# Cross-attention with image prompts: the gram by balanced column strips, the queries two chunks at once with a contraction split in row halves

## The chip, the cores and the metric

The kernel runs on one core of a Trainium2 chip. The core has a matrix engine (TensorE, in the profile PE for its matmuls and PEld for its weight loads), a vector engine (VectorE, DVE), a scalar engine (ScalarE, ACT), GpSimd (POOL) and SyncE (SP), which here only starts DMA transfers. TensorE multiplies a stationary tile (the weights) with a moving one and adds into one of eight PSUM banks; a bank has 128 partitions of 512 float32 values each. It can be used as one array of 128x128, as column strips of 64 or 32 columns, or as row strips. The metric is the device time of one execution in microseconds (us).

## What is computed

Eight batches of 112 rows with 320 channels attend, with 20 heads of 16 channels, to 371 text tokens of 512 features, and beside these to 4 prompt tokens, whose logits get the cosine between the text that a row attended to and the prompt. Everything is float32.

```python
q = heads(hidden_states @ W_q)
k_t = heads(text_ehs @ W_k)
v_t = heads(text_ehs @ W_v)
probs_t = softmax(einsum('bhsd,bhtd->bhst', q, k_t) * attn_scale)
text_out = einsum('bhst,bhtd->bhsd', probs_t, v_t)
attn_scores = einsum('bhsd,bhnd->bhsn', q, heads(ip_ehs @ W_k_ip)) * attn_scale
qsem = l2norm(einsum('bhst,bte->bhse', probs_t, text_ehs))
sem = einsum('bhse,bne->bhsn', qsem, l2norm(ip_ehs))
probs_ip = softmax(attn_scores + 0.5 * sem) * spatial_mask[None, None, :, None]
ip_out = einsum('bhsn,bhnd->bhsd', probs_ip, heads(ip_ehs @ W_v_ip))
out = (text_out + ip_out) @ W_out + b_out + hidden_states
```

## The kernel before

The norm of `qsem` is not taken from `qsem` itself. For each batch the kernel forms the **gram**, the inner products of all 375 tokens with one another (371 text tokens and the 4 normalised prompts), and multiplies the probabilities with it. As the gram is symmetric, only the part on and right of the diagonal is used: it is doubled, and its diagonal blocks are halved again by a table of halves and ones. The gram, one column of ones and 16 channels of values stand side by side in the tile `u`, so that one set of matmuls per head (`product`, L696, the bulk of TensorE's work) gives the squared norm's terms, the prompts' products and the attended values.

A batch takes these steps. `transposed_context` brings the tokens into `ctxT` (features on partitions; for batches after the first VectorE does it, L396, and GpSimd copies the four prompts behind the text, L384). `gram` (L458 to L476) runs over three chunks of 128, 128 and 119 tokens. In each it runs over four slices of the 512 features (e), and for each e over four column strips of TensorE, 32 tokens each. Strip p takes the block q of the chunk that the table `DEAL` gives it. For e = 0 every strip covers the whole width of the chunk's bank (which starts the sums of all columns); for e > 0 only from its own block on. `doubled` copies the bank to the tile `ug` times two with one ScalarE instruction (L454), and GpSimd multiplies the diagonal part with the table `half` (L455). `gram_to_groups` (L482) moves `ug` to `u` by DMA, four transfers for a block, and `values_to_dram` (L558), `values_to_groups` (L567) and `placed` (L614, GpSimd) bring the values beside it through DRAM. `keys` (L494, and L511 for the last 64 channels, in two column halves) and `values` (L533) are projections of the tokens.

`project_queries` serves one batch first (batch 0) and then the pairs [1,2], [3,4], [5,6] and [7]. It transposes x (L331; ScalarE copies it to `xT`, L334; GpSimd fills the unused rows of the last chunk with zeros, L322), and then makes one chunk of 128 channels per step, three steps (L339): three matmuls of 128 rows over 224 columns (112 for a single batch) and two VectorE scalings into `qm` (L348). The contraction has 320 rows, two of 128 and one of 64, filled up with zeros; the third chunk has 64 channels, which stand twice side by side in the weights.

The attention runs in 40 groups, five per batch and four heads each. Scores (L648) run two groups ahead; `probabilities` takes the row maximum on VectorE (L661, `nmx`), the exponential on ScalarE (L665, `p`), the prompts' logits (L667, `ipl`) and sends the result to `xg` by a DMA per head (L672, on SP). `transposed` turns it on VectorE (L684, `xgT`), and `product` multiplies. After that VectorE (L749) and ScalarE (L723) reduce the product's banks.

Groups run in pairs, and in the middle of each pair stands `behind(n)`: there the other work is put into TensorE's queue by hand, a few steps at a time, with one name in the list `turn` for each PSUM bank that these steps use. `qd` is a pool of four banks, shared with the products; `mm` and `sc` have two each. The order of all five engines is the order of the program, nothing is reordered by a scheduler. In the even batches 0, 2, 4 the work of the next pair of queries is spread over three places: in group 2, three transpositions and the first query step between two steps of values; in group 4, the second query step in front of the keys (and for batches 2 and 4 `finish`, `f`, whose output projection is L852 and whose sum into `ob` on VectorE, L858, frees its bank), the gram of the batch after, and the next transposition of x's probabilities, `tr`; in group 1 of the odd batch, the third query step. Batch 6 makes pair [7]: one query step in group 2, two in group 4. Between the two `tr` of a place stand the gram steps in the program, and SP's queue takes the DMAs of all these in the order in which they were issued.

Of the kernel before, what the change touches and what calls it, by code (L numbers as in the profile page):

```python
# [8 lines left out]
F32 = mybir.dt.float32  # L9
# [11 lines left out]
def kernel(  # L21
# [50 lines left out]
    DEAL = ((0, 1, 2, 3), (3, 2, 1, 0), (0, 1, 2, 3))  # L72
# [97 lines left out]
    half = const.tile([P, 2, P], F32, tag="half", name="half")  # L170
# [38 lines left out]
    def more_constants():  # L209
        halves(1)  # L210
        nc.gpsimd.memset(wo_sb[REST:, FULL, :], 0.0)
        for at in attn_ring:
            nc.gpsimd.memset(at[:, C:], 0.0)
# [100 lines left out]
    def project_queries(bs):  # L314
# [7 lines left out]
        nc.gpsimd.memset(xT[REST:, FULL, :], 0.0)  # L322
        for i in range(NC):
            cn = min(P, C - i * P)
            if bs[0] == 0:

                ps = ps_qd.tile([P, 512], F32, tag="qd", name=f"ps_x_0_{i}")
            else:
                ps = bank(f"ps_x_{bs[0]}_{i}", spare=bs[0] > 1 and i > 0)
            for j, b in enumerate(bs):  # L330
                nc.tensor.transpose(  # L331
                    ps[:cn, j * S : (j + 1) * S], x_sb[:, b, i * P : i * P + cn], ident[:S, :S]
                )
            nc.scalar.copy(xT[:cn, i, : n * S], ps[:cn, : n * S])  # L334
            yield
        for i in range(NC):
            ps = bank(f"ps_q_{bs[0]}_{i}")
            for j in range(NC):
                nc.tensor.matmul(  # L339
                    ps[:, : n * S],  # L340
                    wq_sb[:, j, i * P : (i + 1) * P],
                    xT[:, j, : n * S],
                    start=(j == 0),
                    stop=(j == NC - 1),
                )
# [81 lines left out]
    def first_gram():  # L427
# [3 lines left out]
        for c in range(NT):  # L431
# [4 lines left out]
            for r in range(c + 1):  # L436
# [8 lines left out]
                if c == NT - 1:  # L445
                    doubled(banks[r], r, 0)
                yield

    def doubled(ps, c, h):
# [5 lines left out]
        nc.gpsimd.tensor_tensor(g[:, :k], g[:, :k], half[:, h, :k], ALU.mult)  # L455

    def gram(b):
# [3 lines left out]
        for c in range(NT):  # L461
            t0 = c * P
            ps = bank(f"ps_g_{b}_{c}")
            for e in range(NE):
                for p, q in enumerate(DEAL[c]):

                    s0 = q * RG if e > 0 else 0
                    nc.tensor.matmul(  # L468
                        ps[p * RG : (p + 1) * RG, s0 : T - t0],
                        ctxT[:, e, t0 + q * RG : t0 + (q + 1) * RG],  # L470
                        ctxT[:, e, t0 + s0 : T],
# [3 lines left out]
            doubled(ps, c, c % 2)  # L475
# [699 lines left out]
    def behind(n):  # L1175
# [34 lines left out]
        elif b % 2 == 0 and g == 2:  # L1210
            turn[:] = ["qd"] * (6 + (b == 0)) + ["mm"]
# [13 lines left out]
        elif b % 2 == 0 and nb < B - 1:  # L1225
            turn[:] = ["qd"] * (4 + (b > 0)) + ["mm", "mm"]
            turned(b + 2)
            q(nb)
# [15 lines left out]
        elif b % 2 == 0:  # L1244
            turn[:] = ["qd"] * 4 + ["mm"]
            q(nb, 2)
# [181 lines left out]
```

## Time and profile before

| | us |
|---|---|
| median of three runs | 416.45 (415.63 to 416.67) |
| the profiled execution | 416.37 |
| its span in the profile | 414.6 |
| TensorE busy, matmuls | 407.2 |
| VectorE busy | 325.1 |
| ScalarE busy | 188.2 |
| GpSimd busy | 114.0 |

The granted clock of TensorE was 1.0 throughout. The profile takes one execution; its time lies 1.8 us above its span, which counts from the first instruction to the last. In its rows L12 is a line of the kernel, PE ps_g L468 a matmul into the tile ps_g at line 468, and what stands in square brackets is how long the engine stood idle before, and what released it. A row like "4.64 PE ps_g L468 x71" in the chain of waits is a stretch of 4.64 us that the chain spends on 71 such instructions one after another. A float32 matmul is recorded as two instructions of TensorE. Rows of L339 are the queries, L468 the gram, L696 the products, L533 and L494 values and keys.

### The profile page before, as it was taken

To read this page: it belongs to the slowest core of one execution; us is meant where nothing else is said; L and a number is where in the kernel's file an instruction comes from. 1 tells how busy PE (TensorE), PEld (TensorE's weight loads), DVE (VectorE), ACT (ScalarE), POOL (GpSimd) and SP (SyncE) were. 2 spreads that over 40 slices of the span, in tenths; PEclk is the share of its full clock that TensorE was granted. 3 is DMA by queue.
4 is the path that set the end of the run, shared out by engine and by line. 5 is a ranking of instruction groups with operands and counts; after the bars stand their busy time and mean duration, and the time that the engine had idled before them with its cause. 6 is when DMAs were issued, how large, how long until landed. Compare 5 with 4: busy or idle time off the path is not lost.

```text
span 414.6 us, 14048 instructions
## 1 busy us (share of the span) xinstructions
PE 407.2 (98%) x5609; PEld 317.4 (77%) x5609; DVE 325.1 (78%) x694; ACT 188.2 (45%) x652; POOL 114.0 (27%) x266
## 2 busy tenths in 40 slices
PE   8999999999999999999999999999999999999996
PEld 7867777777778786879687877778777878687884
DVE  4256787868888877887898897897888897878975
ACT  3254343336443752515553654333633464336763
POOL 4203112020351351021161135002134126004680
PEclk9999999999999999999999999999999999999999
DMA  7777965986584846578676576566756345666310
GB/s 245 167 197 241 186 167 135 208 196 166 136 184 111 189 117 169 139 167 177 161 164 139 160 158 159 161 167 154 173 147 160 91 123 133 170 151 192 100 48 28
DMA packets 58244, 64.64 MB, mean 156 GB/s; under 512 B 19061, under 2 KB 52041, under 8 KB 58180
## 3 DMA queue, kind: packets, MB, share of 16 engines
q1 hardware_dynamic: 57150, 61.47, 60.3%
q0 software_dynamic: 464, 1.56, 1.7%
q8 instruction: 44, 0.72, 0.8%
q10 hardware_dynamic: 566, 0.72, 0.5%
q14 instruction: 20, 0.16, 0.1%
HBM read 19.03 MB, written 5.22 MB: 59 GB/s over the span
## 4 chain that ended last, share of the span: by engine, by line
PE 95%; DMA 2%; ACT 1%; DVE 1%; POOL 0%; issue 0%; SPq 0%; DVEq 0%
PE ps_qd L696 44%; PE ps_v L533 13%; PE ps_k L494 10%; PE ps_g L468 8%; PE ps_s L648 6%; PE ps_q L339 4%; PE ps_o L852 3%; PE ps_k L511 3%; PE ps_g L438 1%; DMA xg<-p 1%; DMA ct<-in_ctx_dram 1%; PE ps_c L408 1%; PE ps_x L331 0%; POOL shared L738 0%; PE ps_o L948 0%; PE ps_a L843 0%
## 5 line engine op out<-in xcount | busy, mean ns | idle before, releaser
L696 PE MATMUL ps_qd<-u,xgT 32*112 32x40 f32 (+11 forms) x3840 | 217.1, 351 | 1.6 <-DVE xgT L684 1.0
L696 PEld LDWEIGHTS ps_qd<-u,xgT 32*112 32x112 f32 x3840 | 178.1, 172 | 37.7 <-issue 5.5
L684 DVE STREAM_TRANSPOSE xgT<-xg 128x768 f32<-128x768 f32 (+1 forms) x63 | 123.7, 1979 | 11.1 <-DMA xg<-p 9.6
L665 ACT ACTIVATE p<-ps_s,nmx 112x371 f32<-112x371 f32 x160 | 85.7, 585 | 60.8 <-DVE nmx L661 59.5
L661 DVE TENSOR_REDUCE nmx<-ps_s 112x1 f32<-112x371 f32 x160 | 77.3, 535 | 34.8 <-PE ps_s L648 32.8
L614 POOL COPY u<-vr 128x64 f32<-128x64 f32 x120 | 26.9, 237 | 210.7 <-PE ps_qd L696 127.6
L749 DVE CUSTOM_DVE_ANT_0 p<-ps_qd,p 112x371 f32<-112x371 f32 x152 | 73.4, 539 | 13.1 <-ACT pvs L723 8.3
L648 PE MATMUL ps_s<-kT,qm 32*112 32x375 f32 (+1 forms) x320 | 60.9, 485 | 0.0
L533 PE MATMUL ps_v<-wv_sb,ctxT 128*128 128x320 f32 x192 | 56.1, 438 | 0.3 <-ACT kT L501 0.3
L723 ACT COPY pvs<-ps_qd 112x21 f32<-112x21 f32 x152 | 21.8, 198 | 56.3 <-DVE ss L749 49.7
L533 PEld LDWEIGHTS ps_v<-wv_sb,ctxT 128*128 128x128 f32 x192 | 35.3, 190 | 14.7 <-ACT kT L501 1.2
L494 PE MATMUL ps_k<-ctxT,wk_sb 128*128 128x371 f32 x128 | 43.6, 484 | 0.0
L494 PEld LDWEIGHTS ps_k<-ctxT,wk_sb 128*128 128x128 f32 x128 | 23.0, 190 | 13.2 <-issue 1.3
L468 PE MATMUL ps_g<-ctxT 128*32 128x119 f32 (+11 forms) x672 | 33.0, 343 | 0.0
L468 PEld LDWEIGHTS ps_g<-ctxT 128*32 128x32 f32 x672 | 26.2, 109 | 7.4 <-issue 4.6
L648 PEld LDWEIGHTS ps_s<-kT,qm 32*112 32x112 f32 x320 | 27.7, 171 | 5.2 <-ACT p L665 0.4
L396 DVE STREAM_TRANSPOSE ctxT<-ct 128x512 f32<-128x512 f32 x21 | 22.3, 1072 | 6.2 <-DMA ct<-in_ctx_dram 6.2
L540 ACT COPY vext<-ps_v 128x320 f32<-128x320 f32 x24 | 10.2, 426 | 36.3 <-PE ps_v L533 33.9
L667 ACT COPY ipl<-ps_s 112x4 f32<-112x4 f32 x140 | 24.2, 173 | 0.0
L454 ACT ACTIVATE ug<-ps_g 128x375 f32<-128x375 f32 (+2 forms) x24 | 9.1, 378 | 23.3 <-PE ps_g L468 12.5
L455 POOL TENSOR_TENSOR ug<-ug,half 128x128 f32<-128x128 f32 (+1 forms) x24 | 10.6, 449 | 30.3 <-ACT ug L454 30.3
L501 ACT COPY kT<-ps_k 128x371 f32<-128x371 f32 x16 | 7.5, 470 | 22.6 <-PE ps_k L494 22.3
(147 smaller groups left out, 313.5 us busy)
## 6 DMA issues: line engine op xcount, KB each, us to landing
xg<-p SPq DMA_DIRECT2D x159, 162.3 KB
u<-ug SPq DMA_DIRECT2D x128, 99.0 KB
ct<-in_ctx_dram SPq DMA_DIRECT2D x28, 176.0 KB
vip<-vipd SPq DMA_DIRECT2D x7, 560.0 KB
vr<-vd SPq DMA_DIRECT2D x20, 120.0 KB
vd<-vext SPq DMA_DIRECT2D x14, 160.0 KB
vd<-vext SPq DMA_DIRECT2D x28, 40.0 KB
out_dram<-ob SPq DMA_DIRECT2D x7, 140.0 KB
```

Of the source, the lines that this page charges most:

```text
L396: nc.vector.transpose(ctxT[:, :, c * P : (c + 1) * P].rearrange("p e (j i) -> p j e i", i=RG), ct[:, some, :].rearrange("p j (k e) -> p j ...
L468: nc.tensor.matmul(ps[p * RG : (p + 1) * RG, s0 : T - t0], ctxT[:, e, t0 + q * RG : t0 + (q + 1) * RG], ctxT[:, e, t0 + s0 : T], start=(e ...
L494: nc.tensor.matmul(ps[:, :TT], wk_sb[:, e, i * P : (i + 1) * P], s["ctxT"][:, e, :TT], start=(e == 0), stop=(e == NE - 1),)
L533: nc.tensor.matmul(ps[:, :C], ctxT[:, e, c * P : (c + 1) * P], wv_sb[:, e, :], start=(e == 0), stop=(e == NE - 1),)
L614: nc.gpsimd.tensor_copy(region(b, c)[:, :, UV - c * P :], s["vr"][:, c * QN : (c + 1) * QN, g, :])
L648: nc.tensor.matmul(ps[:S, :w], qm[a * RG : (a + 1) * RG, i, r, j * S : (j + 1) * S], s["kT"][a * RG : (a + 1) * RG, i, :w], start=True, st ...
L661: nc.vector.tensor_reduce(nmx, ps[:S, :TT], AX.X, ALU.max, negate=True)
L665: nc.scalar.activation(p, ps[:S, :TT], AF.Exp, bias=nmx)
L667: nc.scalar.copy(s["ipl"][:, groups[g][a], :], ps[:S, TT:T])
L684: nc.vector.transpose(xT[:, j : j + n].rearrange("p j (k q) -> p q j k", q=QN), xg[:, :, j * RG : (j + n) * RG].rearrange("p q (j k) -> p ...
L696: nc.tensor.matmul(banks[a][:S, j * RG : UW], xT[a * RG : (a + 1) * RG, j, :S], region(b, c)[a * RG : (a + 1) * RG, p, q * RG :], start=(j ...
L749: nc.vector.tensor_tensor_reduce(out=p, in0=ps[:S, :TT], in1=p, scale=1.0, scalar=0.0, op0=ALU.mult, op1=ALU.add, accum_out=s["ss"][:, h : ...
```

## The change

There are two parts.

*The gram.* Every strip now starts at its own block for e = 0 as well, so no strip covers columns left of its block, and `DEAL` gives the blocks of the second and third chunk to other strips. Since the columns left of a strip's block are no longer written, `doubled` copies in four pieces: the columns that all strips have, with all partitions, and three pieces of 32 partitions for what is left of them. The table `half` has a slice for each chunk in place of two. The first batch's gram has no strips and keeps the single copy, under the name `doubled_whole`. With the other order of blocks the values of a batch go to DRAM in 1 + 3 + 2 transfers for the three chunks, in place of 1 + 4 + 1.

*The queries of the pairs.* The first two chunks are made in one step, in two banks: two full matmuls for each, and then the last 64 rows of the contraction as two matmuls with 64 rows, the upper half of the array's rows for one bank and the lower half for the other. For this the last 64 rows of the weights and of `xT` are there twice, in both partition halves: GpSimd copies the weights once, ScalarE copies `xT` once per pair, and the fill with zeros is left out. The third chunk is made for both batches of the pair side by side: each batch has its own column half of the array, 64 channels by 112 columns, with its own row half for the last 64 rows, and VectorE scales it with four instructions over 64 partitions and 112 columns in place of two over 128 and 224. For the single batch of the last pair only the last contraction is cut to 64 rows.

As two chunks are now one step, the step in group 4 goes: group 2 makes both chunks (seven `qd` banks in `turn` in place of six), group 4 begins with the step that followed. For pair [7] the third chunk is made there alone.

```diff
-    DEAL = ((0, 1, 2, 3), (3, 2, 1, 0), (0, 1, 2, 3))
+    DEAL = ((0, 1, 2, 3), (3, 2, 0, 1), (1, 2, 3, 0))
...
     def more_constants():
         halves(1)
+        nc.gpsimd.tensor_copy(wq_sb[REST:, FULL, :], wq_sb[:REST, FULL, :])
+        halves(2)
...
             nc.scalar.copy(xT[:cn, i, : n * S], ps[:cn, : n * S])
+            if i == FULL and bs[0] > 0:
+                nc.scalar.copy(xT[REST:, i, : n * S], ps[:REST, : n * S])
             yield
+        both = []
         for i in range(NC):
             ps = bank(f"ps_q_{bs[0]}_{i}")
+            if i < FULL and bs[0] > 0:
+                both.append(ps)
+                for j in range(FULL):
+                    nc.tensor.matmul(
+                        ps[:, : n * S],
+                        wq_sb[:, j, i * P : (i + 1) * P],
+                        xT[:, j, : n * S],
+                        start=(j == 0),
+                        stop=False,
+                    )
+                if i < FULL - 1:
+                    continue
+                for m, ps in enumerate(both):
+                    own = slice(m * REST, (m + 1) * REST)
+                    nc.tensor.matmul(
+                        ps[:, : n * S],
+                        wq_sb[own, FULL, m * P : (m + 1) * P],
+                        xT[own, FULL, : n * S],
+                        start=False,
+                        stop=True,
+                    )
...
+            if i == FULL and bs[0] > 0 and n > 1:
+                w = n * S // 2
+                for j in range(NC):
+                    for h in range(2):
+                        k = slice(h * REST, (h + 1) * REST) if j == FULL else slice(P)
+                        nc.tensor.matmul(
+                            ps[h * REST : (h + 1) * REST, :w],
+                            wq_sb[k, j, FULL * P : C],
+                            xT[k, j, h * w : (h + 1) * w],
+                            start=(j == 0),
+                            stop=(j == NC - 1),
+                        )
...
             for j in range(NC):
+                k = slice(REST) if j == FULL and bs[0] > 0 else slice(P)
...
+    def doubled(ps, c, deal=DEAL[0], h=0):
...
+        common = (QN - 1) * RG
+        nc.scalar.mul(g[:, common:], ps[:, common : T - t0], 2.0)
+        for p, q in enumerate(deal):
+            if q < QN - 1:
+                own = slice(p * RG, (p + 1) * RG)
+                nc.scalar.mul(g[own, q * RG : common], ps[own, q * RG : common], 2.0)
+        nc.gpsimd.tensor_tensor(g[:, :k], g[:, :k], half[:, h, :k], ALU.mult)
...
     def gram(b):
...
                 for p, q in enumerate(DEAL[c]):
-
-                    s0 = q * RG if e > 0 else 0
                     nc.tensor.matmul(
-                        ps[p * RG : (p + 1) * RG, s0 : T - t0],
+                        ps[p * RG : (p + 1) * RG, q * RG : T - t0],
                         ctxT[:, e, t0 + q * RG : t0 + (q + 1) * RG],
-                        ctxT[:, e, t0 + s0 : T],
+                        ctxT[:, e, t0 + q * RG : T],
...
         elif b % 2 == 0 and g == 2:
-            turn[:] = ["qd"] * (6 + (b == 0)) + ["mm"]
+            turn[:] = ["qd"] * (7 + (b == 0)) + ["mm"]
...
         elif b % 2 == 0 and nb < B - 1:
-            turn[:] = ["qd"] * (4 + (b > 0)) + ["mm", "mm"]
+            turn[:] = ["qd"] * (3 + (b > 0)) + ["mm", "mm"]
             turned(b + 2)
-            q(nb)
...
         elif b % 2 == 0:
-            turn[:] = ["qd"] * 4 + ["mm"]
-            q(nb, 2)
+            turn[:] = ["qd"] * 3 + ["mm"]
+            q(nb)
```

37 lines of the change are left out of this document (29 added, 8 removed).

## The prediction

> **What bounds the kernel now.** I read the page's table of engines and its chain of work that ended last, then that chain as a list in order of time, then the groups by shape, and at last the timelines of three stages.
>
> ```profile
> PE 407.2 (98%) x5609; PEld 317.4 (77%) x5609; DVE 325.1 (78%) x694; ACT 188.2 (45%) x652; POOL 114.0 (27%) x266
> ...
> PE 95%; DMA 2%; ACT 1%; DVE 1%; POOL 0%; issue 0%; SPq 0%; DVEq 0%
> PE ps_qd L696 44%; PE ps_v L533 13%; PE ps_k L494 10%; PE ps_g L468 8%; PE ps_s L648 6%; PE ps_q L339 4%; PE ps_o L852 3%; PE ps_k L511 3%; PE ps_g L438 1%; DMA xg<-p 1%; DMA ct<-in_ctx_dram 1%; PE ps_c L408 1%; PE ps_x L331 0%; POOL shared
> ```
>
> TensorE is the path: 95% of the chain and 407 of 414.6 us. A us taken off PE is a us off the kernel, unless PE then stands waiting for what the other engines deliver. The change touches the gram (8%) and the queries (4%). Their stages, from the chain in order of time (start, duration):
>
> ```profile
> 31.46 4.64 PE ps_g L468 x71
> ...
> 61.90 1.14 PE ps_q L339 x6
> 63.03 2.15 PE ps_v L533 x8
> ...
> 75.88 1.33 PE ps_q L339 x6
> ...
> 80.31 4.64 PE ps_g L468 x69
> ...
> 89.97 0.41 issue
> ...
> 97.33 1.33 PE ps_q L339 x6
> 98.66 1.40 PE ps_k L511 x15
> ...
> 117.76 2.35 PE ps_v L533 x8
> ...
> 355.76 0.66 PE ps_q L339 x6
> ...
> 369.28 1.52 PE ps_q L339 x12
> ```
>
> Each matmul is two instructions ("passes"). Eight passes of 320 columns take 2.15 us, so a column costs 2.15/2560 = 0.84 ns. A query pass of 224 columns is 1.14/6 = 0.19 us, one of 112 columns 0.66/6 = 0.11. The same work right after work in another tile shape is dearer: 1.33 against 1.14, 2.35 against 2.15. **A change of tile shape** into 128x128 thus costs 0.19 to 0.20 us. Into the 64-column shape of the last keys: 8 turns of 186 columns at 0.84 ns are 1.25, the row says 1.40, so 0.15.
>
> **The gram (seven times, five of them not in the list above, all 4.64).** The group of its widest pass:
>
> ```profile
> L468 PE MATMUL ps_g<-ctxT 128*32 128x375 f32 x98 | 18.9, 485 | 0.0
> ```
>
> 98 = 7 x 14: four strips x two passes of the first e at the full width, and 3 x 2 more of strip 0. Adding each strip's own passes over the three chunks, strip 0 is longest before: 8 x 375, then 2 x 247 + 6 x 151, then 8 x 119, 5352 columns or 4.50 us; with 0.14 for the shape this is the measured 4.64. Had each set of four passes waited for its widest, it would be 8 x (375 + 247 + 119) = 5928 columns, 4.98 us, which is more than the row. So strips run ahead of one another and the longest sum decides. Afterwards strips 0 and 3 have 8 x (375 + 151 + 87) and 8 x (279 + 215 + 119), both 4904 columns. That is 448 columns, 0.38 us, less: **7 x 0.38 = -2.6 us**.
>
> What it adds is on ACT: four copies in place of one.
>
> ```profile
> L454 ACT ACTIVATE ug<-ps_g 128x119 f32<-128x119 f32 x8 | 2.2, 270 | 3.5 <-PE ps_g L468 2.6 <-PE ps_g L438 0.5 <-POOL attn L213 0.4
> L282 ACT COPY kv<-ps_kv 32x160 f32<-32x160 f32 x1 | 0.3, 284 | 0.0
> L667 ACT COPY ipl<-ps_s 112x4 f32<-112x4 f32 x140 | 24.2, 173 | 0.0
> ```
>
> The last chunk's 0.27 us becomes four of between 0.17 and 0.28, some 0.9 us. Its bank is wanted again by the second pair of scores, over a us into the products, except in the prologue, where a score of the first pair takes it: between 0 and 0.7 us, once. I take 0.1, as ACT is 45% busy and copies back to back overlap at their ends.
>
> **The queries of pairs [1,2], [3,4], [5,6].** They have three places, shown for the first pair; the other two have the same lengths 98 and 196 us later.
> - Stage of group 2 (61.90): 6 passes become 8 full ones and, for the two K = 64 ends, 2 turns of two passes side by side: 10 x 0.19. The 64-row shape has no row here. Below, its entry is free; above, it costs what 128x128 costs, 0.20. I take 0.19, since all shape changes measured lie at 0.15 to 0.20. The values behind it pay their way back, 2.35 for 2.15. So 1.90 + 0.19 + 0.20 - 1.14 = +1.15. That the row halves run at once is seen only of 32-row strips: the page's group of products has 3840 passes of 351 ns in 217 us of busy time. If the two halves went one after the other, it is 0.38 more.
> - Stage of group 4 (75.88): the step goes, the shape change stays with what follows: 0.19 - 1.33 = -1.14.
> - Next batch, group 1 (97.33): 6 passes of 0.19 plus entry become six turns of 112 columns, two at once in column halves, as the last keys' passes are (16 in 1.40): 6 x 0.11 and two shape changes of 0.1 to 0.15, 0.87. So -0.46; between -0.7 (changes free) and 0 (halves in turn).
>
> Together -0.45 each, **-1.4**. Pair [7] pays the same switches over 112 columns: 0.66 becomes 10 x 0.11 + 0.19 and +0.2 behind it (+0.8), the 1.52 of twelve passes becomes 6 x 0.11 and two or three switches (-0.4): **+0.4**. PE alone: **-3.6 us**.
>
> Beside the path: DVE's scalings of the third chunk go from 2 to 4 instructions, the extra ACT copy of xT's tail replaces a POOL fill and has the 2.15 us of values ahead of the queries as cover, and the values go out in six DMAs per batch as before.
>
> ```profile
> L348 DVE TENSOR_SCALAR qm<-ps_q,emask 128x224 f32<-128x224 f32 x18 | 7.2, 445 | 2.7 <-PE ps_q L339 2.7
> L348 DVE TENSOR_SCALAR qm<-ps_q,emask 128x112 f32<-128x112 f32 x12 | 3.3, 326 | 5.1 <-PE ps_q L339 5.1
> ```
>
> 4 x 0.33 - 2 x 0.45 = 0.4 us of DVE, with the keys and values of 100 to 107 us over it.
>
> **What is given back.** In the stage of group 4 the change takes 1.14 + 0.38 = 1.5 us of PE work away, and that work covers a chain of softmax rows, DMAs, transpositions and the output sum. Its length does not change; it starts from scores made just after the group 2 stage, which now ends 1.15 us later. First batch, SP's queue, then DVE and PE:
>
> ```profile
> 55.64 4.05 SPq L672 DMA_DIRECT2D xg<-p  x4
> ...
> 79.48 3.66 SPq L672 DMA_DIRECT2D xg<-p  x4
> 83.19 2.07 SPq L136 DMA_DIRECT2D ct<-in_ctx_dram  x4
> ```
>
> ```profile
> 87.35 1.58 DVE L684 STREAM_TRANSPOSE xgT<-xg 128x768 f32<-128x768 f32 x1 [3.44 <-DMA xg<-p]
> ...
> 89.67 0.57 ACT L665 ACTIVATE p<-ps_s,nmx 112x371 f32<-112x371 f32 x1 [4.30 <-DVE nmx L661]
> ...
> 90.39 1.06 PE L696 MATMUL ps_qd<-u,xgT 32*112 32x392 f32 x5 [0.41 <-POOL u L614]
> ```
>
> SP issues without a pause from 55.64 to 85.26 (the first, eighth and last of nine groups), so the xg data that DVE waits 3.44 us for does not come earlier. Behind that transposition stand the row maxima, and the exponential behind them (to 90.24) frees a bank of the products at 90.39; the row names POOL, whose copy was done earlier. PE is idle there already (89.97, 0.41). PE's lead there is 0.38 (first gram) - 1.15 + 1.14 + 0.38 = 0.75, and I count 0.7 as lost.
>
> Third batch:
>
> ```profile
> 165.97 4.26 SPq L672 DMA_DIRECT2D xg<-p  x4
> ...
> 176.30 3.65 SPq L672 DMA_DIRECT2D xg<-p  x4
> ```
>
> ```profile
> 178.64 0.59 POOL L614 COPY u<-vr 128x64 f32<-128x64 f32 x3 [8.89 <-DMA xg<-p]
> ...
> 179.17 0.20 POOL L384 COPY ctxT<-ipnT 128x16 f32<-128x16 f32 x1
> 179.64 4.71 PE L468 MATMUL ps_g<-ctxT 128*32 128x375 f32 x96
> ...
> 182.46 1.71 DVE L684 STREAM_TRANSPOSE xgT<-xg 128x768 f32<-128x768 f32 x1 [0.68 <-DMA xg<-p]
> ...
> 184.00 0.50 DVE L858 TENSOR_TENSOR ob<-ps_o,xb 112x320 f32<-112x320 f32 x1
> 184.28 1.25 PE L696 MATMUL ps_qd<-u,xgT 32*112 32x392 f32 x10
> ```
>
> The gram needs the prompt copy (179.37), queued on POOL behind copies that wait for a DMA; PE would be there at 179.64 - 1.14 = 178.50, so 0.87 is waited. The products of heads 2 and 3 need the bank that ob's sum frees at 184.50, behind a transposition that waits for SP's transfer; the remaining 0.64 goes there. All 1.5 lost.
>
> Fifth batch:
>
> ```profile
> 276.07 0.80 DVE L348 TENSOR_SCALAR qm<-ps_q,emask 128x224 f32<-128x224 f32 x2
> 276.75 4.88 DVE L684 STREAM_TRANSPOSE xgT<-xg 128x1536 f32<-128x1536 f32 x2
> 281.44 0.50 DVE L858 TENSOR_TENSOR ob<-ps_o,xb 112x320 f32<-112x320 f32 x1
> ...
> 282.33 1.22 PE L696 MATMUL ps_qd<-u,xgT 32*112 32x392 f32 x10
> ```
>
> Here DVE's two transpositions run back to back behind the removed scalings, and can start up to 0.68 earlier. ob is free at 281.94, or 281.26 if the transfers keep up; the products would start at 282.33 - 1.5 = 280.8. That is 0.45 to 1.1 lost; I take 0.75.
>
> Sum: -3.6 + 0.7 + 1.5 + 0.75 + 0.1 = -0.55 on the profiled execution's 416.37 us: **415.8**. The median of the runs, 416.45, is the same within 0.1.
>
> **Rivals.**
> 1. *The cover isn't needed.* SP's row at 165.97 follows scores of PE, so a faster PE may pull the whole chain. For it: outside these stages SP's largest wait is for ACT, 63.4 us in 51 waits (row below), behind PE's scores. Against: the three stages' rows above. Without the 2.95 given back: 412.9.
>
> ```profile
> SPq L672 <- ACT ipl L667: 63.4, 51, 8.1
> ```
>
> 2. *The strips don't run further ahead.* Strip 3 now leads strip 0 by 8 x 96 columns after the first chunk, before by 6 x 96. If the lead is capped at rounds of four, old and new gram cost alike: PE -1.0; with 1.14 less cover instead of 1.5, 0 + 1.1 + 0.45 + 0.1 comes back: about +0.65, 417.0. The 4.64 against 4.98 speaks against it.
> The Trainium skill (TensorE: Matmul & The Clock Gate, Part 3) says that matmuls start strictly in program order; by that rule this rival holds. The trace's 4.64 us disagrees with it.
> 3. *Slower: the row halves.* If the 64-row passes of the two banks go one after another (0.38) and each way through the shape waits out a whole pass (the row below, 0.36, in place of 0.19: 0.35 for both), every pair's group 2 stage costs 0.73 more, pair [7] 0.5: 2.7 us in all, 418.5; with the first half alone 417.2. It outweighs the forecast's gain from 0.15 us extra per pair. Against it: 32-row strips do run at once.
>
> ```profile
> L339 PE MATMUL ps_q<-xT,wq_sb 128*128 128x224 f32 x54 | 12.3, 364 | 0.0
> ```
>
> The Trainium skill (TensorEngine Tiling (Array Packing), Key Properties) says that changing the tiling mode drains TensorE, the tile alone not. The 0.15 to 0.20 us above agree in kind; the page gives no price.
>
> **How the numbers follow.** Forecast 0.55, rival 1 0.20, rival 2 0.11, rival 3 0.14. The forecast's own range, from the given-back bounds (fifth batch 0.45 to 1.1, first 0 to 0.75), the prologue (0 to 0.7) and the shape changes (free: -0.4 x 3), not all at one end together, is 414.4 to 417.0. 0.3%, 1.25 us, is about what a measurement of this kernel can tell from none. Faster by more: nearly all of rival 1 and a quarter of the forecast, 0.34. Slower by more (over 417.6): half of rival 3, a quarter of rival 2, and 0.10 of the forecast's 0.55 for waits that no row here shows, 0.20. The rest, 0.46. The range reaches toward rival 1 and into rival 3: 413.2 to 417.8.
>
> **What would show it.** In the new profile: grams of 4.26; queries of 2.1 us at the first place with values of 2.35 behind; 0.87 at the third; at the group 4 stages a gap ahead of the third batch's gram and ahead of heads 2 and 3. Grams of 4.64 mean rival 2, 2.5 us at the first place rival 3, no such gaps rival 1. The prediction is wrong if PE waits in stages where it now has no gap.

## The result, and the profile after

The changed kernel takes 419.15 us in the median of 14 runs (417.18 to 422.89), the kernel before 416.42 us in 14 runs beside it (414.98 to 418.26). The ratio is 1.0076, with a 95% interval of 1.0054 to 1.0098: slower by 2.2 to 4.1 us, where 0.6 us less were forecast. The profiled execution took 420.84 us, with a span of 419.1. Medians and ratios, here and below, leave out one execution each of e_turn and e_best that ran in a slower state.

The page of the changed kernel, first the engines, then the clock by slices, then the chain:

```profile
PE 409.5 (98%) x5627; PEld 320.0 (76%) x5627; DVE 328.3 (78%) x700; ACT 200.1 (48%) x719; POOL 114.3 (27%) x268
...
PEclk9999899999999999999999999999999999999999
...
PE 95%; DMA 3%; ACT 1%; POOL 0%; issue 0%; SPq 0%; DVE 0%; POOLq 0%; ACTq 0%
```

TensorE is as busy as before, and the DMAs have a larger part in the chain. In one slice, near 50 us, the granted clock is not full. The chain in order of time, at the places that were shown of before (start, duration; the queries' lines are now L347 for full passes, L358 for the row halves, L377 for the column halves, L396 for the old form; the gram is L536, the products L764):

```profile
37.53 10.32 DMA wip<-in_L_xattn_W_v_ip_dram
47.90 2.35 PE ps_kv L275 x28
...
67.55 1.51 PE ps_q L347 x8
69.06 0.58 PE ps_q L358 x4
69.64 2.35 PE ps_v L601 x8
...
85.97 4.58 PE ps_g L536 x62
...
101.85 0.87 PE ps_q L377 x12
...
140.69 4.58 PE ps_g L536 x62
...
279.74 1.33 DMA xg<-p
281.35 0.59 POOL u L682 x3
282.13 4.65 PE ps_g L536 x63
...
360.03 0.88 PE ps_q L347 x8
360.91 0.41 PE ps_q L358 x4
...
374.36 1.03 PE ps_q L396 x6
```

The queries are what was forecast: 1.51 + 0.58 = 2.09 at the first place (2.09 = 1.90 + 0.19), values of 2.35 behind, 0.87 at the third place. The gram is not: 4.58, where 4.26 was forecast. Two things were not foreseen at all. The prompt projection (L275) waits for its weights until 47.9 us, and then takes 2.35 us for 28 of its 32 passes. Before, all 32 took 1.23, without a wait:

```profile
43.81 1.23 PE ps_kv L273 x32
```

The windows of the changed kernel (stretch, its length in us, busy time with the count of instructions of PE, PEld, DVE, ACT and POOL in this order, granted clock, DMA share, GB/s) show why it is slow as well as late:

```profile
42.00:45.00 3.00, 3.00 (x43) 2.17 (x35) 3.00 (x8) 0.41 (x4) 0.47 (x2) 1.00 0.94 191
45.00:48.00 3.00, 0.70 (x9) 0.25 (x12) 0.46 (x2) 0.43 (x1) 0.00 (x0) 0.96 1.15 181
48.00:51.00 3.00, 3.00 (x36) 1.75 (x40) 0.00 (x0) 0.67 (x3) 0.07 (x1) 0.50 0.58 126
```

TensorE stood still for most of the second stretch, busy for 0.70 of 3.00 us, and then ran at a granted clock of 0.50.

A second profile of the changed kernel (label "again" below, an execution of 418.44 us) does not have this wait. The two profiles against that of before, stage by stage: each number says how much longer TensorE took from the start of the stage to the start of the next one.

| us more than before | first profile | second profile |
|---|---|---|
| until the gram of the prologue | +0.74 | +0.98 |
| the seven grams | -0.42 | -0.42 |
| the products behind the prologue's gram | +0.70 | +0.70 |
| the prompt projection and the products behind it | +4.28 | 0 |
| queries and the values behind them | -0.96 | -0.96 |
| first batch, products of the group 4 stage | -1.09 | -1.34 |
| third batch, wait ahead of the gram and products | +0.47 | +0.75 |
| fifth batch, the same | +0.97 | +1.41 |
| from the last projections to the end | -0.23 | +0.96 |
| sum | +4.46 | +2.08 |

The first row is the landing of the first loads, whose code is the same in both kernels. In the last row the second profile holds 1.7 us for the last output transfer, which took 4.6 us from the last sum to the end of the span in place of 2.9. Both differ from one execution to the next: in the profiles of the experiments below the first gram starts 0.1 us earlier to 1.3 later than before, and the last transfer took 4.6 us in e_best too.

### The profile page after: what moved, and what is told of

Its sections match the earlier page's. It is cut to its first block, busy times and chain, and to the rows that moved or that the text cites. A ratio compares the mean times of both kernels' runs of the same rounds, so it can differ in the third digit from the quotient of the medians.

```text
span 419.1 us, 14178 instructions
## 1 busy us (share of the span) xinstructions
PE 409.5 (98%) x5627; PEld 320.0 (76%) x5627; DVE 328.3 (78%) x700; ACT 200.1 (48%) x719; POOL 114.3 (27%) x268
## 4 chain that ended last, share of the span: by engine, by line
PE 95%; DMA 3%; ACT 1%; POOL 0%; issue 0%; SPq 0%; DVE 0%; POOLq 0%; ACTq 0%
PE ps_qd L764 45%; PE ps_v L601 13%; PE ps_k L562 10%; PE ps_g L536 8%; PE ps_s L716 6%; PE ps_k L579 3%; DMA wip<-in_L_xattn_W_v_ip_dram 2%; PE ps_o L920 2%; PE ps_q L347 1%; PE ps_g L495 1%; PE ps_w L482 1%; PE ps_q L396 1%; PE ps_c L465 1%; PE ps_q L377 1%; PE ps_kv L275 1%; PE ps_a L911 1%
## 5 line engine op out<-in xcount | busy, mean ns | idle before, releaser
L764 PE MATMUL ps_qd<-u,xgT 32*112 32x136 f32 (+11 forms) x3840 | 217.4, 352 | 0.9 <-POOL u L682 0.8
L764 PEld LDWEIGHTS ps_qd<-u,xgT 32*112 32x112 f32 x3840 | 179.8, 172 | 35.5 <-issue 5.6
L536 PE MATMUL ps_g<-ctxT 128*32 128x375 f32 (+11 forms) x672 | 32.6, 334 | 0.5 <-POOL ctxT L441 0.5
L536 PEld LDWEIGHTS ps_g<-ctxT 128*32 128x32 f32 x672 | 27.9, 110 | 6.0 <-issue 1.6
L899 POOL TENSOR_TENSOR wv<-vip,w 112x1280 f32<-112x1280 f32 (+1 forms) x8 | 17.5, 2184 | 0.0
L517 POOL TENSOR_TENSOR ug<-ug,half 128x128 f32<-128x128 f32 (+1 forms) x21 | 9.4, 450 | 29.0 <-ACT ug L516 29.0
```

Source lines behind the costliest of these rows:

```text
L536: nc.tensor.matmul(ps[p * RG : (p + 1) * RG, q * RG : T - t0], ctxT[:, e, t0 + q * RG : t0 + (q + 1) * RG], ctxT[:, e, t0 + q * RG : T], s ...
L764: nc.tensor.matmul(banks[a][:S, j * RG : UW], xT[a * RG : (a + 1) * RG, j, :S], region(b, c)[a * RG : (a + 1) * RG, p, q * RG :], start=(j ...
```

## The experiments

All medians stand beside those of the kernel before on the same chip. The ratios are to before, with their 95% intervals; they are those of the record, and need not equal the quotient of the two medians.

| kernel | median us | before | ratio |
|---|---|---|---|
| e_gram, the gram's part alone | 417.8 | 416.31 | 1.0032 (1.001 to 1.0053) |
| e_query, the queries' part alone | 419.17 | 416.31 | 1.0058 (1.0028 to 1.0088) |
| e_order, changed, gram in another order | 418.76 | 416.31 | 1.0054 (1.0024 to 1.0084) |
| e_turn, changed, other banks in the prologue | 418.84 | 416.31 | 1.0046 (1.0013 to 1.0079) |
| e_third, before, third query chunk alone | 415.77 | 417.08 | 0.9991 (0.9963 to 1.0019) |
| e_cover, changed, third chunk in group 4 | 418.61 | 416.58 | 1.0049 (1.0022 to 1.0076) |
| e_pieces, before, doubling in pieces | 416.95 | 416.82 | 0.9995 (0.9967 to 1.0022) |
| e_strip2, before, ordered strips, other banks | 416.84 | 416.61 | 1.0012 (0.9987 to 1.0037) |
| e_best, ordered strips and third chunk | 415.6 | 416.58 | 0.9987 (0.9959 to 1.0014) |

### The two parts by themselves

The gram's part: the table DEAL, the strips from their own block, the pieces of `doubled`.

> The gram's part of the change alone, with the queries as before. Theory (a strip can lead the others by about two passes only): grams of 4.58 us as in the changed kernel, so 7 x 0.06 gained; the prologue's products behind the first gram 6.06 in place of 5.36 (four ScalarE pieces hold the bank), so +0.3 us in all if the prompt projection does not wait for its weights, 416.7 us, and up to +3 more in executions where it does. Rival (the gram's part is harmless, the loss sits in the queries): prologue 5.4 and 416.0 or less. Rival (the load of the prompt weights was late by chance): the projection does not wait here and the whole is within 0.3 us of before.

Its profile has grams of 4.58, products of 6.06 behind the prologue's gram and no wait at the projection. The time is 417.8, 0.4 to 2.2 us more than before, in which the 0.3 us of the theory lies just outside. The gram's part is not harmless, by this interval.

The queries' part: the two-chunk step, the column halves and the placement.

> The queries' part alone, with the gram as before. Theory: 2.19, nothing, 0.87 us at the three places as in the changed kernel, so 1.0 us less for TensorE, of which the waits at the stages of group 4 take back about 1.4 (third batch 0.4, fifth batch 1.0), less what the first batch's gap loses: 416.0 to 417.0, no 0.7 in the prologue, no wait at the prompt projection. Rival (the queries' part makes the whole loss): 418.5 to 419.5 with gaps ahead of products that the kernel before does not have.

419.17, 1.2 to 3.7 us more than before, and above what the theory allowed; that is the rival's range. In this profile the projection takes 2.6 us longer than before, 1.96 of them with TensorE idle, which neither expectation had. The losses of the two parts, 1.5 and 2.9 us by the medians, do not add up to the whole's 2.7. The chain of e_query at the row halves of the second pair, and at the fifth batch:

```profile
166.85 0.58 PE ps_q L357 x4
...
281.26 1.34 DMA xg<-p
282.68 0.59 POOL u L670 x3
283.46 4.71 PE ps_g L524 x71
```

The gram of the fifth batch stands behind GpSimd's copy, and that behind a transfer, as with the whole change.

### How far a strip can lead

```diff
-        for c in range(NT):
...
-            for e in range(NE):
-                for p, q in enumerate(DEAL[c]):
...
+        order = []
+        for p in range(QN):
+            t = 0
+            for c in range(NT):
+                for e in range(NE):
+                    order.append((t, c, e, p))
+                    t += T - c * P - DEAL[c][p] * RG
...
+        ps = [bank(f"ps_g_{b}_{c}") for c in range(NT)]
+        for _, c, e, p in sorted(order):
...
```

> The changed kernel with the gram's matmuls put in the queue in the order in which their strips come free, over all three chunks. Theory (in a queue in program order a strip leads by about two passes at most): each gram 4.26 to 4.30 in place of 4.58, so 7 x 0.3 = 2.1 us less for TensorE; at the stages of group 4 the three grams' part may be waited off, so 1.2 to 2.1 less than the changed kernel, 417.0 to 418.0. Rival (a floor for narrow passes or the weight loads bound the gram): 4.55 to 4.6 as before the reordering, and no gain.

The chain of this kernel:

```profile
139.07 4.26 PE ps_g L542 x62
...
181.78 4.26 PE ps_g L542 x62
...
275.62 2.83 DMA vr<-vd
278.73 0.59 POOL u L690 x3
279.51 4.33 PE ps_g L542 x62
```

The same matmuls, queued in the order in which their strips come free, take 4.26 us in place of 4.58. So it is the queue. (The edit also claims the gram's three banks ahead of its first matmul, and makes the gram one step of the program in place of three.) In the trace of the changed kernel the start of single passes shows it (third gram of the first profile: us from the gram's start, strip, columns; the passes of strips 1 and 2 in between are left out where the dots stand):

```
2.130 strip 2 247
2.140 strip 3 215
2.229 strip 0 375
...
2.544 strip 0 151
...
2.563 strip 3 215
```

Strip 3 is at its tenth pass at 2.140, when strip 0 begins its eighth at 2.229. Its eleventh, free to start about 0.2 us later, starts only at 2.563, right behind the start of strip 0's ninth. A strip leads by two passes and then stands until the slowest has taken its next one. The new deal asks for a lead of 8 x 96 columns, 0.65 us or nearly three passes of 279 columns. In the trace of before strip 3 stood in the same way, but for 0.06 us only, and strip 0 was the longest there.

The time did not follow: 418.76, where 417.0 to 418.0 was expected. In this profile the products behind the third and fifth gram, and those of two later stages (at 303 and 375 us), stand 0.4 to 0.9 us longer than before. Its projection took 1.6 us longer too, and its prologue's products 6.31 us. What the order gives, the waits of this execution take; whether they come from the order, from the banks or by chance is not shown.

### The bank in the prologue

```diff
-    turn[:] = ["mm", "mm", "sc"]
+    turn[:] = ["sc", "mm", "mm"]
     run(("g", 1), lambda: gram(1), NT)
```

> The changed kernel with the banks of the prologue's gram dealt the other way: its first chunk takes the bank that the coming scores share, the last two those of the projections. Theory (the four ScalarE pieces of the last chunk free that bank late): the products behind it 5.36 to 5.5 us in place of 6.06, so 0.6 less. Rival (scores wait for ScalarE or VectorE for another reason): 6.0 or more as now. For the prompt projection's wait for its weights: if it comes from the change's later start it shrinks at most by nothing, as TensorE comes sooner; if it is chance it may be gone.

The changed kernel's timeline behind the prologue's gram, ScalarE's pieces first, then TensorE's products and scores:

```profile
36.24 0.30 ACT L512 ACTIVATE ug<-ps_g 128x151 f32<-128x151 f32 x1 [0.24 <-PE ps_g L536]
36.55 0.70 ACT L516 ACTIVATE ug<-ps_g 32x32 f32<-32x32 f32 x3
37.27 0.19 ACT L512 ACTIVATE ug<-ps_g 128x23 f32<-128x23 f32 x1
37.36 0.68 ACT L516 ACTIVATE ug<-ps_g 32x64 f32<-32x64 f32 x3
```

```profile
36.72 0.93 PE L764 MATMUL ps_qd<-u,xgT 32*112 32x392 f32 x8
37.48 1.17 PE L716 MATMUL ps_s<-kT,qm 32*112 32x371 f32 x3
...
42.78 2.42 PE L601 MATMUL ps_v<-wv_sb,ctxT 128*128 128x320 f32 x8
```

with the other banks:

```profile
35.86 1.22 PE L764 MATMUL ps_qd<-u,xgT 32*112 32x392 f32 x10
36.63 0.48 PE L716 MATMUL ps_s<-kT,qm 32*112 32x371 f32 x2
...
41.31 2.42 PE L601 MATMUL ps_v<-wv_sb,ctxT 128*128 128x320 f32 x8
```

and before:

```profile
36.03 1.22 PE L696 MATMUL ps_qd<-u,xgT 32*112 32x392 f32 x10
...
41.39 2.42 PE L533 MATMUL ps_v<-wv_sb,ctxT 128*128 128x320 f32 x8
```

In the changed kernel the pieces run to 38.04, and the second score, which wants the last chunk's bank, stands for them: from the products' start to the values it is 42.78 - 36.72 = 6.06 us. With the other banks it is 41.31 - 35.86 = 5.45, and before 41.39 - 36.03 = 5.36. The term is shown, at 0.6 to 0.7. The median, 418.84, did not fall clearly by it: the intervals of the two ratios overlap.

### The pieces of the doubling alone

The kernel before with `doubled` in four pieces; strips, order and queries as they were.

> The kernel before with the doubling in four pieces alone: strips, their order and the queries as before (all columns are written, the pieces only leave out what nobody reads). Theory (the pieces make the gram part's loss: they hold the bank in the prologue and stand ahead of exponentials later): grams 4.64, the prologue's products 6.06, 417.2 to 418.0 in the median. Rival (they cost nothing but the prologue's 0.7): 416.8 to 417.2. Rival (the loss is in the strips' new deal or the order of the value transfers): 416.3 to 416.7.

416.95 beside 416.82, though its prologue's products take 5.99 us in place of 5.36: the first batch's group 4 stage waits 0.4 us less, and the rest goes unseen in the spread. So the pieces by themselves are not seen to make the gram part's loss, though the intervals of e_pieces and e_gram overlap from 1.001 to 1.0022. That points at the new deal, with the other order of the value transfers that it brings, as the last rival had it. These two were not told apart, and neither was changed alone.

### The queries without the missing step

The kernel before with the third chunk alone in column halves, and both first chunks in their old places:

> The kernel before with the third query chunk alone made in column halves; the first two chunks as before, one step in group 2 and one in group 4, so the cover of the group 4 stages stays whole. Theory (the waits there come from the step that the change took away): 0.87 us in place of 1.33 at three places and no new wait at the group 4 stages, 1.4 us less than before, 414.9. Rival (what PE gains is waited off at the next stage in any case, wherever it is gained): 416.0 or more with gaps as in the changed kernel.

Its chain at the three places and around the grams of the third and fifth batch:

```profile
176.36 1.33 PE ps_q L366 x6
...
182.11 4.64 PE ps_g L495 x71
186.75 1.15 PE ps_qd L723 x10
...
197.72 0.87 PE ps_q L347 x12
...
279.67 4.64 PE ps_g L495 x71
284.31 1.15 PE ps_qd L723 x10
...
370.72 1.70 PE ps_q L366 x12
```

The grams follow without a gap, and the products behind them start with the 1.15 us of an undisturbed stage. The third chunk takes 0.87 as in the changed kernel. 415.77 lies between the theory's 414.9 and the rival's 416.0, without the rival's gaps. It is 1.3 us below the median beside it, though the interval (0.9963 to 1.0019) does not tell it from before. It does tell it from the queries' whole part: 1.0028 to 1.0088 lies wholly above. What separates the two is the step that makes two chunks at once and leaves group 4 without one. By TensorE's stages that step costs 0.2 us (at pair [7]; at the other pairs it only moves work); the medians differ from their befores by -1.3 and +2.9.

Giving the stage of group 4 another step back:

```diff
         elif b % 2 == 0 and nb < B - 1:
-            turn[:] = ["qd"] * (3 + (b > 0)) + ["mm", "mm"]
+            turn[:] = ["qd"] * (4 + (b > 0)) + ["mm", "mm"]
             turned(b + 2)
+            q(nb)
...
         elif g == 1:
-            turn[:] = ["qd"] * 4 + ["mm"]
+            turn[:] = ["qd"] * 3 + ["mm"]
             gram_to_groups(nb, (2,))
-            q(b)
```

> The changed kernel with the third query chunk of a pair moved from group 1 of the next batch into the group 4 stage, where the change had taken the second chunk's step away; nothing else. Theory (the gaps at the group 4 stages are lost cover): TensorE's work is the same, the stage is longer by 0.87 us, and the gaps ahead of the third and fifth batch's gram and in the products behind go by up to that, about 1.5 us in all; the later places lose nothing as they have no gap. 417.5 to 418.5. Rival (the gaps come from transfers and transpositions that are late by as much wherever PE stands): gaps as before, 419.

418.61. The wait ahead of the fifth batch's gram is gone, but the products behind the third and fifth stand 0.5 and 0.8 us longer than before, and others at 306 us 1.1 us. The interval overlaps that of the changed kernel. With 0.87 us of work put back, the waits moved more than they went: this does not settle how much of the loss is cover.

### The weights of the prompt projection

These are three ways to take the projection's wait away by moving something: the load some 20 us earlier, in the changed kernel and in the kernel before, and the projection one step of values later.

> The changed kernel with the two prompt weights loaded some 20 us earlier (their DMAs ahead of the first batch's gram transfers). Theory (the wait of the prompt projection for these weights, 0 to 3.8 us from one execution to the next, makes a large part of the loss): the projection 1.22 us without a wait, the spread of the times as narrow as before's, the median 1 to 2 us less than the changed kernel's 419.1. Rival (the wait only moves: what follows waits as long for SP's or DVE's chain): the median stays at 419, with the time back in the products behind the projection or at the first batch's stage of group 4.

> The kernel before with the same earlier load. Theory (the kernel before hides that load with some 0.6 us to spare, and in a part of its executions not): 0 to 0.5 us less in the median, the executions of 419 and 420 us gone. Rival (its long executions come from elsewhere): no change, 416.3 with the same spread.

> The changed kernel with one more step of the next batch's values ahead of the prompt projection (from the group 2 stage of the first batch), which so comes 2.2 us later, with the weights' load where it was. Theory (the projection waits for these weights 0 to 2.6 us, and past about 2.5 us the granted clock falls to one half for some us): the projection 1.22 us, no fall of the clock, the executions above 420 gone, the median 0.5 to 1.5 us less than the changed kernel's. Rival (the wait is made up later, since the products behind it wait for VectorE anyway): no change in the median, the time back in the products behind the projection.

All three made it worse: 424.04 (ratio 1.0191), 419.46 (1.0072) and 421.23 (1.0101). With the earlier load the projection takes 1.22 us without a wait, but the scores' and the gram's transfers stand behind 1.3 MB of weights, and the prologue's gram and the products behind it take 1.9 us more in the kernel before and 4.5 more in the changed one, there in part at a granted clock of 0.51. The later projection is also 1.22, and the 2.15 us of values missing in the group 2 stage come back as waits there and at the first batch's gram. Five of its nine executions show a granted clock of 0.994 to 0.996. None of the theories held, and the rivals' times were too low as well: the wait moves, and costs more where it goes.

So the load itself was halved, with every step of TensorE in its place (the prompt values are then not those of the reference):

```diff
-            for i, w in enumerate((wkip_sb, wvip_sb)):
+            for i, w in enumerate((wkip_sb, wkip_sb)):
...
-    load_embed(nc.sync, wvip_sb, w_v_ip)
```

> The kernel before with one of the two prompt weights left out (the key weights are used for both products, so the prompt values are not the reference's; the number of instructions of TensorE is the same and 0.64 MB less is loaded). Theory (the kernel before hides the load in most executions): 0 to 0.5 us less than before, without the executions above 419. Rival (its load costs as much as the changed kernel's): 1 us less or more.

> The changed kernel with the same weights left out. Theory (the wait for these weights makes about half of the loss): no wait at the projection, no fall of the clock, 417.5 to 418.0, so 1.2 to 1.9 us above the kernel before with the same left out. Rival (the wait is nearly all of the loss): within 0.5 us of it. Rival (the wait is made up later): 418.7 or more.

> The queries' part alone with the same weights left out. Theory: 1.0 us less of TensorE, 0.8 to 1.0 waited at the first batch's group 4 stage, 0.2 to 0.4 at the third's, 1.3 at the fifth's, so 1.2 to 1.6 above the kernel before with the same left out. Rival (the queries' part loses only by the weights' wait): the same as it, or less.

415.75 (ratio 0.998, 0.9963 to 0.9997), 418.44 (1.0052) and 416.8 (1.0007), each to the full kernel before. The kernel before gains 0.9 us by its median and the changed one 0.7 (its interval overlaps that of the full changed kernel), and the difference between them stays: 418.44 - 415.75 = 2.7 us. So the wait for the weights costs the two about alike in the middle of their executions, and it is not what separates them. The fall of the clock isn't either: the 11 of the 14 executions of the changed kernel with a mean granted clock of 0.998 or more have a median of 418.9, against 416.4 before. The queries' part alone is another case. It gains 2.4 us (419.17 to 416.8, with ratios whose intervals do not overlap), so most of that part's loss goes with this load; what is left is 1.05 us above the kernel before without it.

### Everything that should help, and the changed kernel again

> All that should help together: the kernel before, with the balanced strips queued in the order in which they come free, the other banks for the prologue's gram, the third query chunk in column halves and the earlier load. Theory: grams of 4.28 (7 x 0.36 = 2.5 less), 1.4 less in the queries, prologue as before; the group 4 stages lose 0.36 of cover and may wait that off: 3 to 4 us less than before, 412.5 to 413.5. Rival (each gain is waited off): above 415.5.

This is 418.55 (1.0045), with the earlier load in it. The next three leave the load where it was: e_best has pair [7] as before too, e_strip2 the ordered strips alone, and e_bestlate is e_best with the later projection.

> The kernel before with the balanced strips queued in the order in which they come free, the other banks for the prologue's gram, and the third query chunk of the three full pairs in column halves (pair [7] as before); the load where it was. Theory: 7 x 0.36 + 3 x 0.46 = 3.9 us of PE less, of which the products behind the first, third and fifth batch's gram may take back 1: 413.0 to 414.0. Rival (every gain is waited off): 416.

> The kernel before with the balanced strips queued in the order in which they come free and the other banks in the prologue; queries and load as before. Theory: 7 x 0.36 = 2.5 us of TensorE less, of which the products behind the gram at the group 4 stages take back at most 1: 414.3 to 415.2. Rival (waited off): 416.3.

> The kernel of e_best with the prompt projection 2.2 us later as in e_late. Theory (its wait costs the kernel of e_best some of its executions too): 0.3 to 1 us less than e_best, with a narrower spread. Rival: as e_best or more, since the group 2 stage of the first batch is 2.2 us shorter and loses that cover.

They take 415.6, 416.84 and 417.98. The first is the best mixture found, 2.5 us less of TensorE's work in the grams and 1.4 in the queries, and its interval (0.9959 to 1.0014) still does not tell it from before. 2.5 us less in the grams alone bring nothing that shows. In e_bestlate (ratio 1.0028, 0.9989 to 1.0066) the six executions with a mean granted clock of 0.990 to 0.996 took 418.55 to 421.06 us, the other six 415.44 to 417.4. No version with the reference's results beats the kernel before clearly.

> The changed kernel as it is, for a second profile. Theory: grams 4.58, queries 2.19, 0 and 0.87, prologue 6.06 as in the first; the wait at the projection anywhere from 0 to 3 us; the first batch's group 4 stage 0.8 to 1.0 over before's where the projection did not wait, the third's and fifth's 0.4 and 1.0 over it. Rival (the stages behind differ from one execution to the next by as much as the projection): other gaps than in the first profile, in stages where neither kernel had one.

This second profile shows the forecast's wait at the third batch as it described it. At the fifth there is one of the same kind ahead of the gram, where the forecast had only the wait for `ob`. The timeline at the two batches:

```profile
179.10 0.59 POOL L682 COPY u<-vr 128x64 f32<-128x64 f32 x3 [8.42 <-DMA vr<-vd]
179.63 0.20 POOL L441 COPY ctxT<-ipnT 128x16 f32<-128x16 f32 x1
...
179.89 4.65 PE L536 MATMUL ps_g<-ctxT 128*32 128x375 f32 x96 [0.49 <-POOL ctxT L441]
...
184.42 0.46 DVE L926 TENSOR_TENSOR ob<-ps_o,xb 112x320 f32<-112x320 f32 x1
...
184.93 0.47 PEld L764 LDWEIGHTS ps_qd<-u,xgT 32*112 32x112 f32 x8 [0.19 <-DVE ob L926]
```

```profile
277.70 0.59 POOL L682 COPY u<-vr 128x64 f32<-128x64 f32 x3 [8.81 <-DMA vr<-vd]
278.23 0.20 POOL L441 COPY ctxT<-ipnT 128x16 f32<-128x16 f32 x1
...
278.49 4.65 PE L536 MATMUL ps_g<-ctxT 128*32 128x375 f32 x96 [0.88 <-POOL ctxT L441]
```

The gram waits for the prompt copy on GpSimd, the copy stands behind three that wait for a DMA, and the products of the later heads wait for `ob`.

## Why the prediction was wrong

*The step that failed first: the gram, 7 x 0.38 = 2.6 us.* It measured 7 x 0.06 = 0.42. The argument took from 4.64 against 4.98 that the longest strip's own sum decides. It holds only while the longest strips need not lead the others by more than two passes. Before, the longest was strip 0, which led none; in the new deal strip 3 is one of the two longest and needs a lead of nearly three. The second rival named this and got 0.11. It set the cap at no gain, which is nearly what came, and its time was 417.0. The row that could have told the two apart, the start of single passes of one strip, was not read. That the queue's order is the cause is shown: another order of the same matmuls gives 4.26.

*The queries: right to 0.04 us at each stage of the three full pairs,* the 64-row shape at 0.19 and the row halves at once included. The third rival falls.

*What is given back: right in place at the third batch, and its sum for the third and fifth near in size in the second profile alone* (2.25 forecast, 1.44 and 2.16 in the two profiles, with the fifth's larger and the third's smaller than forecast). The first batch's 0.7 went the other way in both profiles, -1.09 and -1.34: the kernel before already waits there, and the changed one waits less. In the profiles of e_turn and e_query 0.7 and 1.0 us were lost there. That TensorE comes late and finds the wait done does not explain this: it came to that gram 5.7 and 1.6 us later than before in the two profiles, and 4.8 us later in e_query. So this term differs between executions, one number for it was wrong, and its cause stays open.

*The prologue's bank: 0.1 taken, 0.70 measured,* the upper end of its bound. The reason given for the low end, ScalarE's small share of busy time, was no reason: the bank's next user stands right behind.

*The range and the chances.* They had no room for what an execution adds by chance, the projection's wait and the fall of the clock behind it. But the halved load shows that both kernels pay for the wait.

With the gram at its measured size and the prologue at 0.7 the forecast's own sum becomes -0.55 + 2.2 + 0.6 = +2.25 us, the lower end of the measured 2.2 to 4.1. But this is not the account. A gram that is only 0.06 us shorter also takes less cover away, 1.2 us and not 1.5; counted as rival 2 counts it, the sum is -1.4 for TensorE, + 1.1 + 0.45 for the third and fifth batch, + 0.7 for the prologue, so +0.85. Nor did restoring the gram's 2.1 us restore the time (418.76 against 419.15). And the two profiles of the changed kernel, without the rows that differ by chance (start, projection, last transfer), come to 0.6 to 0.8 us below before, or 0.3 to 0.7 above if the first batch's row is left out with them. So beneath the mis-sized terms lies an assumption that failed too: that what TensorE saves outside the three stages reaches the end, and that one execution shows where it doesn't. The kernels with 2.5 and 3.9 us less for TensorE (e_strip2, e_best) stand within 1 us of before. Only the medians say where the loss is made: in the queries, the two-chunk step that leaves group 4 without its own costs more than the column halves, and most of that part's loss by itself goes with the halved load. In the gram they point, without showing it, to the new deal of the strips and not to the pieces of the doubling. Why the whole change is slower by 2.2 us or more stays open, and so does which transfers are late in the executions that no profile here shows.

## What to carry to other kernels

An engine that is busy 98% of the span can still be the last of several chains that end together: before pricing its savings, remove some of its work in one place and see whether the end moves. Work taken from a stage where transfers, copies and a sum run beside it must be counted against their end, and moving the same work to the stage before lengthens the one chain and shortens the cover of the other. Strips that work side by side from one queue in program order are balanced only if none has to run far ahead; put their instructions in the order in which the strips come free. Here that made each gram 0.3 us shorter, though not the whole.

## What the runs showed of the hardware

- Passes in different column strips of TensorE started out of program order in these grams, by up to two passes (one float32 matmul): by the strips' sums the gram is 4.26 us, queued in rounds it took 4.58, in order of need 4.26. The Trainium skill (TensorE: Matmul & The Clock Gate, Part 3) has matmuls start strictly in program order. This trace disagrees with it up to that lead.
- After a wait of 2.3 us of TensorE the granted clock fell to 0.50 for 3.4 us, and the projection's passes then took 474 ns where they take 299. It fell likewise after waits of 1.96 us (e_query) and 1.82 us (e_bestlate), and did not after 1.58 (e_third), 1.88 (e_early) and 2.05 us (e_all). So no length of wait in this range decides it alone, and the 2.5 us in the expectation of e_late is no limit. The Trainium skill (TensorE: Matmul & The Clock Gate, Part 1) gives one half as the throttled clock and an idle window of about 3.4 us ahead of it. The half agrees; here the shorter waits were enough.
- The load of 0.64 MB for the projection lands in 16 shares, and its last share came 6.4 us after the issue in the kernel before, 6.0 to 9.1 in the other profiles that have this load and 10.3 in the changed one's first profile. There the other 15 were in by 7.0 us. One late share holds up the engine that waits for all.
